# The stages behind attention, reordered by hand in a two-layer attention and expert kernel

## The chip, the cores and the metric

The kernel runs on one core of a Trainium2 chip. The metric is the device time of one execution in microseconds (us), as the median of several runs; lower is better. Engines are called TensorE (PE in the profile; PEld is its weight load), VectorE (DVE), ScalarE (ACT), GpSimd (POOL) and SyncE (SP, which issues most of the DMAs).

## The reference

Four sublayers on x of shape (4, 512, 128), each followed by a residual and a layer norm (cut to the core; biases are kept, small helpers are left out):

```python
# 1: attention with relative positions, 8 heads of 16
score = (einsum(q + u_bias, k) + rel_shift(einsum(q + v_bias, p))) / sqrt(128)
x = layernorm(x + softmax(score) @ v @ Wo + bo)
# 2: eight experts, top 1 (D=128, F=512)
xn = x * rsqrt(mean(x*x) + 1e-6) * rms_w
ye = silu(xn @ W1[e] + b1[e]) @ W2[e] + b2[e]      # e = argmax of xn @ gate_w
x = layernorm(x + ye * max(softmax(logits)))
# 3: gated convolution (3 taps) with a recurrence along the sequence, 256 wide
u = silu(conv(layernorm(x) @ W_in[:, :256])) * sigmoid(gate)
a, b, c = sigmoid(u @ Wa + ba), sigmoid(u @ Wb + bb), tanh(u @ Wc + bc)
state = a_t * state + b_t * u_t ;  y_t = c_t * state + u_t
x = layernorm(x + x + y @ Wo + bo)
# 4: fourteen experts, top 1 (D=128, F=256), gelu
x = layernorm(x + softmax(logits)[e] * (gelu(x @ w1[e] + b1[e]) @ w2[e] + b2[e]))
```

All data is float32.

## The kernel before

The four batches form two groups, (0, 1) and (2, 3). Tokens lie on the partitions in four tiles of 128 per batch, or, transposed, features on the partitions and 512 tokens along the free dimension. A float32 matmul takes two passes of TensorE, a transpose one.

**Attention** (function `attention`, L936) goes through 64 steps of two heads: scores (L643), softmax (L661 to L670), the flip of the probabilities one step or two later (L678, L680), and the product with V (L691). The engines' order in this part is the order of the program (`tc.manual_schedule`). Other work is cut into generators in the list `side`; each step calls each of them twice, and `room` says how many PSUM banks the step may lend them. `tiles_end` (L697) normalises and projects a pair of tiles, `attn_end` (L734) does the layer norm, the RMS norm, the routing and, for the last batch of a group, the dispatch. `experts(0, 0, ...)`, the layer-0 experts of the first group, is appended at step 49.

**Routing** (`route`, L277) takes the logits (L292), the largest, an Exp for the shares (L300) and the choice. **Dispatch** (L332) counts the tokens of each expert with matmuls (L354 to L356), gives each token a slot and writes the rows to their slots in DRAM (`sent`) with one indirect DMA of GpSimd per tile of 128 tokens (L386). A group of 1024 tokens has a block of 128 slots for each expert and 7 overflow blocks, whose expert is known only on the chip: 15 blocks in layer 0, 21 in layer 1.

**Experts** (L765) load blocks of rows in sets of four (L799), transpose them (L807), and for each block do an up projection (L822), bias (L829), the nonlinearity (layer 0: Tanh at L835 and a product at L842, layer 1: Gelu at L838), a down projection (L852) and a copy (L861); a set of four goes to DRAM (`made`, L864). Weights come through the tile `wd` (L787): 6 buffers with 4 loads ahead for the first group in layer 0, 3 and 3 for all others; 512 KB a block in layer 0. In layer 1 the weights of the fourteen experts are kept on the chip (`w1p`, `w2p`) and only overflow blocks load.

**Behind attention** no order is written out for the engines: the program calls one function after the other (L1133 to L1143), and the framework schedules its instructions. `layer0_end` (L1033) gathers the results with four indirect DMAs per batch (`collect`, L1023), takes two normalisations in a row, each with its own power on GpSimd (`rsqrt_of`, L229), and transposes. `recurrence` (L1060) does the convolution (L1071), its Sigmoid (L1073), the gate (L1076, L1078), the three gates of the recurrence (L1087, L1089), the scan (L1091), the output projection (L1098) and the routing of layer 1. `layer1_end` gathers and writes the output.

```python
    for b in GROUPS[0]:
        layer0_end(b)
    in_turns(recurrence(0), recurrence(1))
    drain(experts(1, 0, mid, None, None, W1_0, W2_0, E0, F0, "b1_0", col("rms_w")))
    drain(dispatch(0, x3, E1, F1, "b1_1", 1))
```

Batches 2 and 3 follow in the same way, then `second(0)`, a dispatch and `second(1)`, the layer-1 experts of each group with their ends.

Of the kernel before, what the change touches and what calls it, by code (L numbers as in the profile page):

```python
# [63 lines left out]
def tile_kernel(ctx: ExitStack, tc: tile.TileContext, x, wpack, cols, rows, tabs, b2bd0, b2bd1,  # L64
# [10 lines left out]
    small = pool(ctx, "small", 3)  # L75
# [7 lines left out]
    psum_a = pool(attn_psum, "psum_a", 1, **psum_of)  # L83
    prep_ctx = ExitStack()
    even = pool(prep_ctx, "even", 1)
# [50 lines left out]
    minus_half = const.tile([P, NT], F32, name="minus_half")  # L136
# [21 lines left out]
    def later_constants():  # L158
# [11 lines left out]
        def counting(name, pattern, base=0, channel_multiplier=0):  # L170
            shape = [P, *(n for _, n in pattern)]
            whole = const.tile(shape, I32, name=f"{name}i")
            nc.gpsimd.iota(whole, pattern=pattern, base=base, channel_multiplier=channel_multiplier)
            t = const.tile(shape, F32, name=name)
            nc.gpsimd.tensor_copy(t, whole)
            return t
# [13 lines left out]
    now, room = [None], [0]  # L190

# [31 lines left out]
    def rsqrt_of(src, n, eps, name, engine=None):  # L223

        engine = engine or nc.vector
        v = small.tile([P, n], F32, tag=f"var{n}", name=f"var_{name}")
        engine.tensor_scalar(v, src, eps, None, ALU.add)
        y = small.tile([P, n], F32, tag=f"rstd{n}", name=f"rstd_{name}")
        nc.gpsimd.tensor_tensor(y, v, minus_half, ALU.pow)  # L229
        t = small.tile([P, n], F32, tag=f"root{n}", name=f"root_{name}")  # L230
        engine.tensor_tensor(t, y, y, ALU.mult)
        engine.tensor_tensor(t, t, v, ALU.mult)
        engine.tensor_scalar(t, t, -0.5, 1.5, ALU.mult, ALU.add)
        engine.tensor_tensor(y, y, t, ALU.mult)
        return y

# [9 lines left out]

    def stats_of(src, name, engine=None):

        mean, var = moments(src, name)
        return mean, var, rsqrt_of(var, NT, 1e-5, name, engine)  # L250
# [14 lines left out]
    def transposed(src, name):  # L265

        pt = ps(name)
        for n in range(NT):
            nc.tensor.transpose(pt[:, n * P : (n + 1) * P], src[:, n, :], ident)  # L269
        return pt  # L270
# [4 lines left out]
    chosen, shares, slots, extra = {}, {}, {}, {}  # L275

    def route(xT, weights, n_e, b, layer, out):  # L277
# [4 lines left out]
        if at == 0:  # L282
            n_t = len(GROUPS[gr]) * NT
            chosen[layer, gr] = plan.tile([P, n_t, n_e], F32, tag=f"chosen{layer}_{gr}", name=f"chosen{nm}")
        mine = chosen[layer, gr][:, at : at + NT, :]
        w = small.tile([P, NT, 32], F32, tag="w", bufs=2, name=f"w{nm}")
# [4 lines left out]
        for n in range(NT):  # L291
            nc.tensor.matmul(lg[:, n, :], lhsT=xT[:, n * P : (n + 1) * P], rhs=weights, start=True, stop=True)  # L292
        yield
# [6 lines left out]
        nc.scalar.activation(ex, ex, AF.Exp)  # L300
# [3 lines left out]
        nc.vector.tensor_tensor(mine, eq, over(first, n_e), ALU.is_equal)  # L304
        yield
        yield
# [8 lines left out]
    def b2_of(w, b2t, b, layer, dst, base):  # L315
# [4 lines left out]
        nc.tensor.transpose(pw, w.rearrange("p n e -> p (n e)"), ident)  # L320
        yield
        wT = small.tile([P, P], F32, tag="wT", bufs=2, name=f"wT{nm}")
        nc.scalar.copy(wT, pw)
        yield
        yield from bank()
        pb = ps(f"pb{nm}")
        nc.tensor.matmul(pb, lhsT=wT, rhs=b2t, start=True, stop=True)
        yield
# [3 lines left out]
    def dispatch(gr, rows_of, n_e, n_f, b1, layer):  # L332
# [10 lines left out]
        eq = chosen[layer, gr]  # L343
        yield

        cum = brief("cum", [P, GT + 1, n_e], f"cum{nm}")
        nc.vector.memset(cum[:, 0, :], 0.0)
        for n in range(GT):
            nc.vector.tensor_tensor(cum[:, n + 1, :], cum[:, n, :], eq[:, n, :], ALU.add)
        yield  # L350
# [5 lines left out]
        nc.tensor.matmul(flat, lhsT=ones, rhs=cum[:, :GT, :].rearrange("p n e -> p (n e)"), start=False, stop=True)  # L356
        rank = flat.rearrange("p (n e) -> p n e", e=n_e)
# [16 lines left out]
        yield  # L374
        yield
# [7 lines left out]
        yield  # L383
# [10 lines left out]
        yield  # L394

# [7 lines left out]
        yield  # L403
        yield
# [12 lines left out]
        yield  # L417
# [59 lines left out]
    def attn_prep(b):  # L477
# [9 lines left out]
        apply_norm(xh, xs[b], mean, rsqrt_of(var, NT, 1e-5, f"a{b}", engine), engine)  # L487
# [106 lines left out]
        yield  # L594
# [5 lines left out]
    right_keys = [odd_even.tile([P, NG, S], F32, name=f"KR{i}") for i, odd_even in enumerate((even, odd))]  # L600
# [96 lines left out]
    def tiles_end(b, t2):  # L697
# [32 lines left out]
        if t2 == 1 and b < B - 1:  # L730
            side.insert(0, attn_end(b))
        yield

    def attn_end(b):  # L734

        engine = nc.vector if b == B - 1 else nc.gpsimd
        x1[b] = keep.tile([P, NT, D], F32, tag="x1", name=f"x1_{b}")
        yield
        mean, var, rstd = stats_of(xs[b], f"b{b}", engine)
        apply_norm(x1[b], xs[b], mean, rstd, engine)  # L740

        ms = small.tile([P, NT], F32, tag="ms", name=f"ms{b}")
        engine.tensor_tensor(ms, var, rstd, ALU.mult)
        engine.tensor_tensor(ms, ms, rstd, ALU.mult)
        rr = rsqrt_of(ms, NT, 1e-6, f"r{b}", engine)
        xf = keep2.tile([P, NT, D], F32, tag="xf", bufs=len(GROUPS[0]), name=f"xf{b}")
        xf_of[b] = xf
        for n in range(NT):
            engine.tensor_scalar(xf[:, n, :], x1[b][:, n, :], rr[:, n : n + 1], None, ALU.mult)
        for _ in range(4):  # L750
            yield
        yield
# [5 lines left out]
        yield  # L758
        w = []
        yield from route(xfT[b], colr("gate"), E0, b, 0, w)  # L760
        if b == GROUPS[GROUP[b]][-1]:
            yield from dispatch(GROUP[b], xf_of, E0, F0, "b1_0", 0)
        yield from b2_of(w[0], b2t0, b, 0, x1[b], x1[b])

    def experts(gr, layer, mid, w1t, w2t, W1, W2, n_e, n_f, b1, scale):  # L765
# [10 lines left out]
        def take(j):  # L776
# [10 lines left out]
            wd = mid.tile([P, 2 * n_f], F32, tag=f"wd{layer}", bufs=6 if within else 3, name=f"wd{nm}_{j}")  # L787
# [8 lines left out]
        def fetch(s):  # L796
            js = sets[s]
            rows_[s] = mid.tile([P, n_set, D], F32, tag="rows", name=f"rows{nm}_{s}")
# [3 lines left out]
        def turn(s):  # L802
# [3 lines left out]
            for k in range(len(js)):  # L806
                nc.tensor.transpose(pt[:, k * P : (k + 1) * P], rows_[s][:, k, :], ident)  # L807
            return pt

        def turned(s, pt):  # L810
            n = len(sets[s]) * P
            xts[s] = mid.tile([P, n_set * P], F32, tag="xt", name=f"xt{nm}_{s}")
# [5 lines left out]
        def up(j):  # L818
            xt = xts[j // n_set]
            ups[j] = ph = experts_psum("ph", f"ph{nm}_{j}")  # L820
# [4 lines left out]
        def bent(j):  # L825
            ph = ups.pop(j)
            hb = mid.tile([P, nf, P], F32, tag=f"hb{layer}", bufs=4 if within else 3, name=f"hb{nm}_{j}")
# [18 lines left out]
        def down(m):  # L846
            js = range(m * n_down, min((m + 1) * n_down, nblocks))
            py = experts_psum("py", f"py{nm}_{m}")
# [6 lines left out]
            def then():  # L855
                s = sets[js[0] // n_set]
                if js[0] == s[0]:
                    ys[js[0] // n_set] = mid.tile([P, n_set, D], F32, tag="ys", name=f"ys{nm}_{m}")
# [9 lines left out]
        ahead = 4 if within else 3  # L868
# [48 lines left out]
        yield  # L917
        yield
        yield from run(ops)

    def drain(gen):
        for _ in gen:
            pass
# [3 lines left out]
    side = []  # L927
# [8 lines left out]
    def attention(first, last):  # L936

        for k in range(first, last):
# [32 lines left out]
            if due is not None and due[2] == 1 and due[1] % 2 == 1:  # L971
                side.insert(0, tiles_end(due[0], due[1] // 2))

    def experts_psum(tag, name):
        return ps(name) if psum_e is None else psum_e.tile([P, 512], F32, tag=tag, name=name)

    psum_e = None
    begun = (B - 1) * NT * H // 2
    by_hand = {mybir.EngineType.PE, mybir.EngineType.DVE, mybir.EngineType.Activation, mybir.EngineType.Pool}
    with tc.manual_schedule(engines=by_hand):  # L980
# [4 lines left out]
        attention(0, begun + 1)  # L985
    prep_ctx.close()
    first_ctx = ExitStack()
    side.append(experts(0, 0, pool(first_ctx, "first", 2), None, None, W1_0, W2_0, E0, F0, "b1_0", col("rms_w")))
    with tc.manual_schedule(engines=by_hand):
        attention(begun + 1, len(steps) + 6)  # L990
    now[0] = None
    attn_psum.close()
    psum_e = pool(ctx, "psum_e", 3, **psum_of)
    for gen in side:
        drain(gen)
    first_ctx.close()
    mid = pool(ctx, "mid", 2)
    one = pool(ctx, "one", 1)
    drain(attn_end(B - 1))


# [249 lines left out]
```

## Time and profile before

| | us |
|---|---|
| median of 3 runs | 691.08 (687.99 to 693.28) |
| the profiled execution, device time | 696.16 |
| its span, first to last instruction | 694.5 |
| mean granted TensorE clock | 0.858 of full speed |

In the rows of the profile, a number behind x is a count, the first two numbers of a timeline row are start and length in us, and square brackets hold the idle time of the engine before the row and what ended it. In a table of stretches each engine has its busy time and, in brackets, the number of its instructions; then come the granted clock, the DMA engines' busy share and GB/s. Busy times overlap between engines.

### The profile page before, as it was taken

To read this page: it belongs to the slowest core of one execution; us is meant where nothing else is said; L and a number is where in the kernel's file an instruction comes from. 1 tells how busy PE (TensorE), PEld (TensorE's weight loads), DVE (VectorE), ACT (ScalarE), POOL (GpSimd) and SP (SyncE) were. 2 spreads that over 40 slices of the span, in tenths; PEclk is the share of its full clock that TensorE was granted. 3 is DMA by queue.
4 is the path that set the end of the run, shared out by engine and by line. 5 is a ranking of instruction groups with operands and counts; after the bars stand their busy time and mean duration, and the time that the engine had idled before them with its cause. 6 is when DMAs were issued, how large, how long until landed. Compare 5 with 4: busy or idle time off the path is not lost.

```text
span 694.5 us, 11212 instructions
## 1 busy us (share of the span) xinstructions
PE 505.2 (73%) x4060; PEld 352.9 (51%) x4060; DVE 366.3 (53%) x997; ACT 286.2 (41%) x573; POOL 177.9 (26%) x310
## 2 busy tenths in 40 slices
PE   5988979898989859988930797687605894873840
PEld 2455646575666537767920334486602343763830
DVE  2786747655675836573753356345334364342413
ACT  1256545655565635664301332332203333540621
POOL 1572411513141311500157100005053001027014
PEclk9989999989998988999965899578856996896895
DMA  9290131400040070209741000047610000255231
GB/s 321 75 279 16 32 76 16 92 2 1 14 96 1 21 216 24 73 2 246 239 133 60 1 0 0 1 117 219 207 42 0 0 1 0 64 156 150 68 117 53
DMA packets 71366, 56.16 MB, mean 81 GB/s; under 512 B 4624, under 2 KB 64400, under 8 KB 71056
## 3 DMA queue, kind: packets, MB, share of 16 engines
q1 hardware_dynamic: 69264, 51.25, 26.5%
q0 software_dynamic: 2048, 4.20, 1.9%
q8 instruction: 32, 0.52, 0.3%
q14 instruction: 22, 0.18, 0.1%
HBM read 36.30 MB, written 12.58 MB: 70 GB/s over the span
## 4 chain that ended last, share of the span: by engine, by line
PE 45%; DVE 17%; POOL 11%; DMA 8%; issue 8%; ACT 6%; SPq 2%; POOLq 0%; DVEq 0%; ACTq 0%
PE pa L1087 6%; PE py L852 5%; PE ptr L678 5%; PE ph L822 5%; PE ctx L691 4%; DVE nmax L666 4%; PE main L643 4%; PE pj L1071 3%; PE aux L643 3%; POOL back L1023 3%; DMA wd<-in_W_dram 2%; DMA back<-made,at 2%; DVE main L663 2%; DVE main L661 2%; PE pl L292 2%
## 5 line engine op out<-in xcount | busy, mean ns | idle before, releaser
L670 ACT ACTIVATE pr<-main,nmax 128x512 f32<-128x512 f32 x128 | 81.1, 686 | 52.2 <-DVE nmax L666 51.8
L678 PE MATMUL ptr<-ident,pr 128*128 128x128 f32 x512 | 86.5, 294 | 20.4 <-ACT prT L680 5.0
L680 ACT COPY prT<-ptr 128x512 f32<-128x512 f32 x128 | 74.2, 588 | 54.2 <-PE ptr L678 53.4
L678 PEld LDWEIGHTS ptr<-ident,pr 128*128 128x128 f32 x512 | 58.3, 147 | 62.0 <-issue 14.6
L666 DVE TENSOR_REDUCE nmax<-main 128x2 f32<-128x1024 f32 x64 | 78.3, 1224 | 2.2
L661 DVE COPY_PREDICATED main<-low,aux 128x256 f32<-128x256 uint32 x64 | 27.4, 428 | 76.8 <-PE aux L643 75.8
L822 PE MATMUL ph<-xt,wd 128*128 128x128 f32 x296 | 45.3, 299 | 13.3 <-DMA wd<-in_W_dram 12.0
L852 PE MATMUL py<-wd,hb 128*128 128x128 f32 x296 | 45.5, 301 | 5.5 <-ACT hb L838 3.0
L1023 POOL DMA_INDIRECT back<-made,at x32 | 32.7, 1021 | 65.4 <-DMA made<-ys 50.3
L822 PEld LDWEIGHTS ph<-xt,wd 128*128 128x128 f32 x296 | 39.8, 208 | 16.7 <-issue 8.7
L643 PE MATMUL aux<-Ko,QLo 32*128 32x128 f32 x480 | 44.9, 306 | 2.7 <-DMA Ko<-K 2.7
L852 PEld LDWEIGHTS py<-wd,hb 128*128 128x128 f32 x296 | 40.4, 211 | 8.6 <-ACT hb L838 4.5
L1087 PE MATMUL pa<-u,wabct 128*128 128x512 f32 x96 | 41.7, 594 | 1.7 <-ACT sg L1078 1.7
L691 PE MATMUL ctx<-prT,V 128*32 128x128 f32 x1024 | 39.5, 301 | 3.3 <-ACT prT L680 3.3
L269 PE MATMUL pgx<-ident,gxh 128*128 128x128 f32 x16 | 5.1, 451 | 50.1 <-DVE gxh L1045 50.1
L643 PE MATMUL main<-KR,QR 32*128 32x512 f32 (+3 forms) x192 | 40.6, 500 | 0.0
L829 DVE TENSOR_TENSOR hb<-ph,colt 128x256 f32<-128x256 f32 (+1 forms) x44 | 22.8, 519 | 32.5 <-PE ph L822 25.4
L643 PEld LDWEIGHTS aux<-Ko,QLo 32*128 32x128 f32 x480 | 33.1, 194 | 3.5 <-issue 3.5
L691 PEld LDWEIGHTS ctx<-prT,V 128*32 128x32 f32 x1024 | 29.3, 120 | 10.3 <-ACT prT L680 5.4
L386 POOL DMA_INDIRECT sent<-x,at x16 | 16.8, 1048 | 68.9 <-DVE pick L408 39.7
L835 ACT ACTIVATE th<-hb 128x512 f32<-128x512 f32 x30 | 18.9, 630 | 36.9 <-DVE hb L829 35.7
L269 PEld LDWEIGHTS pgx<-ident,gxh 128*128 128x128 f32 x16 | 3.2, 200 | 55.1 <-DVE gxh L1045 53.4
(293 smaller groups left out, 969.3 us busy)
## 6 DMA issues: line engine op xcount, KB each, us to landing
wd<-in_W_dram SPq DMA_DIRECT2D x60, 256.0 KB, 4.8
rows<-sent SPq DMA_DIRECT2D x16, 256.0 KB, 3.2
made<-ys SPq DMA_DIRECT2D x16, 256.0 KB, 2.6
wd<-in_W_dram SPq DMA_DIRECT2D x28, 128.0 KB, 2.3
sent<-zero SPq DMA_DIRECT2D x2, 1344.0 KB, 10.8
tab<-in_tabs_dram SPq DMA_DIRECT2D x2, 1280.0 KB, 9.1
Ko<-K SPq DMA_DIRECT2D x8, 256.0 KB, 4.3
QLo<-QL SPq DMA_DIRECT2D x8, 256.0 KB, 4.0
```

The lines of the kernel that those rows point to most:

```text
L643: nc.tensor.matmul(out, lhsT=Q[r, h // 4, q], rhs=K[r, h // 4, k0:k1], start=True, stop=True)
L661: nc.vector.copy_predicated(main[:, :, c0 : c0 + P], low.bitcast(U32).unsqueeze(1).to_broadcast([P, 2, P]), aux[:, :, 0, :])
L666: nc.vector.tensor_reduce(nmax, main, AX.X, ALU.max, negate=True)
L670: nc.scalar.activation(pr, main[:, i, :], AF.Exp, bias=nmax[:, i : i + 1])
L678: nc.tensor.transpose(ptr[:, c * P : (c + 1) * P], pr[:, c * P : (c + 1) * P], ident)
L680: nc.scalar.copy(prT.rearrange("p c q -> p (c q)"), ptr)
L691: nc.tensor.matmul(pc[32 * i : 32 * i + 32, :P], lhsT=V[:, c, 4 * g + i, :], rhs=prTs[i][:, c, :], start=(c == 0), stop=(c == NT - 1))
L822: nc.tensor.matmul(ph[:, fc * P : (fc + 1) * P], lhsT=weights[j][0][:, fc * P : (fc + 1) * P], rhs=xt[:, j % n_set * P : (j % n_set + 1) * ...
L829: nc.vector.tensor_tensor(hb, ph[:, : nf * P].rearrange("p (c t) -> p c t", t=P), bias.unsqueeze(2).to_broadcast([P, nf, P]), ALU.add)
L852: nc.tensor.matmul(py[:, k * D : (k + 1) * D], lhsT=hT[:, fc, :], rhs=weights[j][1][:, fc, :], start=(fc == 0), stop=(fc == nf - 1))
L1023: nc.gpsimd.indirect_dma_start(out=back[:, n, :], out_offset=None, in_=made[layer, gr][:, :], in_offset=bass.IndirectOffsetOnAxis(ap=slots ...
L1087: nc.tensor.matmul(pa, lhsT=wabct[:, k, kc, i * P : (i + 1) * P], rhs=u[kc], start=(kc == 0), stop=(kc == 1))
```

## The change

- The four compute engines get a written order behind attention too. Generators are given out by `play`: of those that are due, the first in a list always goes on. `spend` counts matmul work as it is given out, and a generator that yields a number rests until that many units were spent.
- Two main streams: `rest_of_last` (end of attention for batch 3, second group's layer-0 experts, its ends, its layer-1 experts), first in the list, and `rest_of_first`. Recurrences and the first group's layer-1 experts are appended behind them, the layer-1 ends are put in front.
- One expert pool `mid` from step 41 on. Weights of layer 0: 4 buffers, 3 ahead; layer 1: 3 buffers, 2 ahead; `rows` one buffer instead of two. The recurrence's tiles take the places of attention's.
- One power for two roots: of var + e and of var(1 + d) + de. The RMS-normed rows come straight from the attention output; they are made on VectorE, the layer-normed rows on GpSimd.
- Sigmoids are written with tanh. The convolution's sum first goes through an Identity on ScalarE; `ga` is halved and shifted on GpSimd. The factors 2 and 4 that this leaves in u go into scales. The Exp of the layer-1 routing becomes a Tanh with a quotient on VectorE.
- The sums over earlier tiles are taken with each batch's routing, the dispatch comes before the shares, and the dispatch of the first group begins the first expert stream itself instead of step 49. `attn_end(1)` stays ahead of `tiles_end` in the list.
- Attention stops 3 steps behind the last scores instead of 6.

```diff
+    def play():
+        while givers:
+            for giver in givers:
+                if giver[0] <= given[0]:
+                    wait = next(giver[1], "end")
+                    if wait == "end":
+                        givers.remove(giver)
+                    else:
+                        giver[0] = given[0] + (wait or 0)
+                    break
+            else:
+                given[0] = min(giver[0] for giver in givers)
...
+    def rstds_of(var, eps, name, engine):
+        v = small.tile([P, 2, NT], F32, tag="var", name=f"var_{name}")
+        engine.tensor_scalar(v[:, 0, :], var, 1e-5, None, ALU.add)
+        engine.tensor_scalar(v[:, 1, :], var, 1.0 + eps, 1e-5 * eps, ALU.mult, ALU.add)
+        y = newton(v, 2, name, engine)
+        return y[:, 0, :], y[:, 1, :]
...
-            wd = mid.tile([P, 2 * n_f], F32, tag=f"wd{layer}", bufs=6 if within else 3, name=f"wd{nm}_{j}")
+            wd = mid.tile([P, 2 * n_f], F32, tag=f"wd{layer}", bufs=(4, 3)[layer], name=f"wd{nm}_{j}")
...
-        ahead = 4 if within else 3
+        ahead = (3, 2)[layer]
...
+        yield from pause(3, sent_at[layer, gr] + 70 - given[0])
...
-            nc.scalar.activation(u[i], pc, AF.Sigmoid, bias=cbias[:, i : i + 1])
-            nc.vector.scalar_tensor_tensor(u[i], pc, cbias[:, i : i + 1], u[i], ALU.add, ALU.mult)
+            nc.scalar.activation(u[:, i, :], pc, AF.Identity, bias=cbias[:, i : i + 1])
+            nc.scalar.activation(sg[:, i, :], u[:, i, :], AF.Tanh, scale=0.5)
+            nc.vector.scalar_tensor_tensor(u[:, i, :], sg[:, i, :], 1.0, u[:, i, :], ALU.add, ALU.mult)
...
+                if k == 0:
+                    nc.gpsimd.tensor_scalar(ga[:, i, :], ga[:, i, :], 0.5, 0.5, ALU.mult, ALU.add)
...
+    def rest_of_last():
+        yield from tiles_end(B - 1, 1)
+        yield from attn_end(B - 1)
+        yield from experts(1, 0, W1_0, W2_0, E0, F0, "b1_0", col("rms_w"))
+        while 1 not in gxs:
+            yield 2
+        backs = [gather(b, 0) for b in GROUPS[1]]
+        yield 40
+        for b, back in zip(GROUPS[1], backs):
+            yield from layer0_end(b, back)
+            while b - 2 not in over_with:
+                yield 2
+            begin(recurrence(b), -1)
+        yield from layer1(1)
+
+    with tc.manual_schedule(engines=by_hand):
+        begin(rest_of_last())
+        begin(rest_of_first([gen for gen in side if gen.__name__ != "tiles_end"]))
+        play()
```

## The prediction

> **What bounds the kernel now.** I read the page first: span 694.5 us, device time of that execution 696.16 us; the three timed runs have the median 691.08 (687.99 to 693.28), 0.7% below it. The sum below is made against the span; 1.7 us lie around it, and at the end I scale by 691.08/696.16 = 0.993.
>
> ```profile
> PE 505.2 (73%) x4060; PEld 352.9 (51%) x4060; DVE 366.3 (53%) x997; ACT 286.2 (41%) x573; POOL 177.9 (26%) x310
> ...
> PE 45%; DVE 17%; POOL 11%; DMA 8%; issue 8%; ACT 6%; SPq 2%; POOLq 0%; DVEq 0%; ACTq 0%
> ```
>
> TensorE holds less than half of the chain that ended last, so the mean tells little. I then had the busy time cut at the borders of the stages (attention's last context matmul ends at 327).
>
> ```profile
> core 0: us, PE busy (x) PEld busy (x) DVE busy (x) ACT busy (x) POOL busy (x), PEclk, DMA share, GB/s
> 0.00:327.00 327.00, 277.88 (x2911) 189.38 (x2915) 202.50 (x430) 171.19 (x315) 93.57 (x212) 0.94 0.31 82
> 327.00:357.00 30.00, 25.09 (x212) 22.46 (x204) 19.43 (x67) 9.16 (x20) 6.65 (x7) 0.94 0.72 213
> 357.00:380.00 23.00, 0.38 (x1) 0.00 (x0) 10.32 (x64) 1.65 (x4) 17.73 (x24) 0.50 0.28 88
> 380.00:430.00 50.00, 42.52 (x120) 20.44 (x120) 25.46 (x54) 17.95 (x27) 2.85 (x6) 0.93 0.00 0
> 430.00:451.00 21.00, 11.15 (x31) 6.79 (x32) 7.40 (x48) 6.67 (x15) 2.44 (x4) 0.54 0.00 1
> 451.00:504.00 53.00, 40.95 (x262) 37.68 (x260) 24.63 (x53) 15.22 (x33) 8.82 (x8) 0.83 0.61 178
> 504.00:530.00 26.00, 1.95 (x7) 1.34 (x7) 12.48 (x62) 4.24 (x10) 15.50 (x20) 0.56 0.10 28
> 530.00:576.00 46.00, 41.60 (x115) 19.40 (x113) 21.90 (x39) 15.65 (x22) 0.00 (x0) 0.95 0.00 0
> 576.00:597.00 21.00, 11.47 (x35) 7.08 (x36) 7.72 (x49) 7.12 (x16) 2.02 (x2) 0.59 0.00 0
> 597.00:623.00 26.00, 22.97 (x191) 21.76 (x190) 12.72 (x42) 15.69 (x48) 2.67 (x3) 1.00 0.45 133
> 623.00:634.00 11.00, 0.08 (x1) 0.00 (x0) 0.64 (x2) 0.28 (x1) 8.34 (x9) 0.65 0.51 157
> 634.00:671.00 37.00, 29.13 (x189) 26.56 (x189) 14.33 (x55) 17.82 (x56) 7.03 (x7) 0.83 0.40 115
> 671.00:694.50 23.50, 0.00 (x0) 0.00 (x0) 6.75 (x36) 3.56 (x9) 10.32 (x10) 0.57 0.17 47
> ```
>
> The reader is to see that the 367 us behind attention go one stage after another. The two recurrences (380 and 530) are dense; between them TensorE is idle or sparse in 357 to 380 and 504 to 530 (rows come back, two normalisations), 430 to 451 and 576 to 597 (x3 and routing), 623 to 634 (scatter, rows). Yet the group of batches 0 and 1 doesn't depend on the other: this idle time is order, not need. Two more views show what sits inside.
>
> ```profile
> 482.84 1.06 PE L852 MATMUL py<-wd,hb 128*128 128x128 f32 x8
> 484.80 1.13 PE L822 MATMUL ph<-xt,wd 128*128 128x128 f32 x8 [0.91 <-DMA wd<-in_W_dram]
> 485.76 1.06 PE L852 MATMUL py<-wd,hb 128*128 128x128 f32 x8
> ```
> ```profile
> 363.34 1.03 POOL L386 DMA_INDIRECT sent<-xf,at  x1 [0.17 <-DVE oneb L414]
> ...
> 372.44 0.98 POOL L386 DMA_INDIRECT sent<-xf,at  x1 [0.30 <-issue]
> 373.42 1.08 POOL L229 TENSOR_TENSOR rstd_c<-var_c,minus_half 128x4 f32<-128x4 f32 x1
> ```
>
> An up and a down projection of a layer-0 block start 0.96 us apart, 1.9 us for both, but a block comes only every 3 us or so (484.80 to the next at 487.87), because it waits for its weights. And POOL issues a burst of eight row DMAs in 10.4 us (1.3 each); the power for a root stood behind such a burst.
>
> **The change, part by part.** *Unit.* The new order counts matmul work. A unit is 0.22 us: a 512-wide fp32 matmul is 4 units and takes two passes of 0.435 (48 passes of the gates in 20.87 us). So its pauses of 35, 40 and 70 units are 7.7, 8.8 and 15.4 us.
>
> *Up to attention's end.* Scatter and expert pool of the first group come some 2 to 4 attention steps earlier (4.6 us each), which takes the wait of 7.2 us for its first rows (at 251.7) out of TensorE's queue; the first normalised rows move from POOL to DVE, 4 x 0.34 us in three batches, +4. The weight ring falls from 6 buffers to 4 while downs come in pairs: up(2m+4) must wait for a load that starts when down(m) ends. The load takes 4.8 us (median of the 256 KB weight loads) plus 0.75 of issue = 5.5. Six pairs, 33 us, if nothing stands between; in attention only about one expert operation goes into a step, so 0 to 2 us remain in each of three pairs, and all of it in the three pairs behind attention. I take +3 in attention, and attention's end unchanged at 327.
>
> *327 to the experts of the second group.* TensorE holds the rest of the first pool, about 7 ups and 13 downs x 0.9 = 18 us, plus up to 15 of ring waits; the second group's normalisation, routing and ranks go between them. The shared root removes one power (1.0 us), its hand-overs and some nine DVE instructions of 0.16 us: about 3 us from this chain, and 2.7 from each normalisation behind layer 0. Pauses of 35, 6 and 10 units lie ahead of the scatter, some 76 units of the rest ahead of the first gather, so by my count the eight scatters now go ahead of the eight gathers: 360 to 370 instead of 363.3 to 373.4. Landing 2.2 and rows 3.2 follow, so this pool begins at 377 (369 to 385). It has strict precedence: the first recurrence, ready at about 380, stands behind it.
>
> *Second pool of layer 0.* Before: 53 us. Now 4 buffers, but down(j-2) follows up(j). A buffer is held for issue and landing (0.7 + 4.0 in this stage), two block periods and 1.9 us of matmuls, and this is four periods: T = 6.6/2 = 3.3 us. 3 x 1.9 + 12 x 3.3 + 2 = 47, to 424. The cover is gone here: what TensorE waits, nobody else uses.
>
> *Recurrences.* 48 + 16 + 96 wide passes stay. Per half, ACT gains one Identity, 0.69 us; DVE has three fused operations of 0.75 where it had 0.75, 0.69 and 0.69; POOL gains one conversion of 128x512. No row shows that one; the copy of this size took 0.61, the two-operand form 1.27, and I take 1.27. All lies beside 45 us of matmuls for two batches (ACT 17, DVE 21, POOL 5). The two-by-two order drops five waits of 0.8 for a sigmoid, so 45 instead of 50 and 42 instead of 46; 4 us of transposes and routing matmuls lie between. Four loads of 1.28 us (sigmoid, exp) go. The gathers and normalisations of batches 2 and 3, 26 us before, now lie beside the first recurrences, and x3 and routing of batches 0 and 1 (21) beside the others. What is late next: a conversion on POOL behind a burst, its scan on DVE, and what is queued behind that scan. Two bursts, each 10.4 us, against slack of two or three steps: I take 3 each, 0 to 10 as bounds. 424 + 45 + 42 + 4 + 6 = 521.
>
> ```profile
> L838 ACT ACT_TABLE_LOAD x1 | 1.3, 1283 | 0.0
> ```
>
> *A rule that speaks against this.* The row shows one load of 1.283 us when Gelu begins; exp loads at 441, and the tanh of the pool behind it (454) needs none, so these two share. Whether tanh after Gelu loads again no row shows; the bounds are 0 and two loads at each alternation, some six alternations, 15 us on ACT. I take 0 on the path, because ACT has 60% idle there.
> The Trainium skill, page "ScalarE: Activation LUTs", section "Table sets: the hidden batching unit", says to do all of one set before the next, and lists tanh with exp and with sigmoid but not with gelu. By that page the sum would have those 15 us more on ACT, and perhaps half of it on the path.
>
> *Last stages.* From the last recurrence to the rows of the second group in layer 1: x3 and routing 21, ranks and DVE 5, scatter 10.4, landing and rows 6, less the overlap with b2, 37. In it the first group's layer-1 pool must fit: 26 before, plus its ring. Three buffers with lag two: from the fourth overflow block on, each takes load 2.3 + issue 0.7 + two projections 0.9 = 3.9 us instead of 2.3, four blocks, +6. So 38, to 559. Then the last pool, 37 before, 4 less for a DVE wait at 641, +5 for the ring: 38, to 597. The end, gathers and norm, stays at 23.5: span 620.5. Plus 1.7, times 0.993: 618 us.
>
> **The rivals.** (a) POOL becomes the bound. 64 row DMAs are 83 us, and three bursts fall into recurrences whose scans now need POOL. Against it: 26% busy. If three bursts come through at 10 us each, +24 beyond my 6: 642, and 655 with a fourth and its gathers.
> (b) The pauses don't fit, and the gaps only move: the order is fixed, so a short pause leaves DVE in front of a gather. Then 26 (504 to 530), 21 (430 to 451) and 23 (574 to 634 is 60, taken as 37) return: 690.5, about 687, no change. For it: gather to rows takes 10.4 + 2.6, more than 8.8. Against it: the next pause follows, and POOL alone is late.
> (c) Slower: the weight ring. Its place is all four pools, 31 refilled blocks, where strict precedence lets nobody fill in, and in the first pool attention's own transposes stand behind the wait. My gain is 74 us, so it decides from 2.4 us a block beyond those I took. At 6.7, the longest landing of the second pool, with six pairs exposed and TensorE at the half clock that it shows from 357 to 380 (0.50), I get 3.5 a block, +108: about 725. Against it: DMA shares of 0.4 to 0.7 leave room, and attention spaces the first pairs.
>
> **How the numbers follow.** Forecast 0.62 (590 to 640); better than 590 by dense matmuls at full clock 0.04; (a) 0.20; (b) 0.05; (c) 0.09. 1% is about what this measurement tells from no change (the runs spread by 0.8%). Faster 0.86, same 0.05, slower 0.09. The range leaves out (b), (c) and the best tail: 590, where ring (3 + 6 + 5), POOL (6) and the late start (8) cost nothing, to 664, (a) with its upper bounds and the half of the first pool's exposed loads.
>
> **What would show it.** Right: second-pool blocks 3.3 us apart with waits for weights; one dense stretch of TensorE of 130 us or more behind it; sparse TensorE only around 355 and in the last 24 us; one power per normalisation; no sigmoid loads. Wrong: gate scans waiting for POOL, gathers seen as DVE's longest wait, weight waits above 5 us inside attention, an activation load at each turn between tanh and Gelu, attention ending past 335.

## The result, and the profile after

The changed kernel takes 721.0 us (median of 4 runs, 719.36 to 723.35) beside 692.18 of the kernel before on the same chip: ratio 1.044, 95% interval 1.038 to 1.050. One of the four runs of the kernel before, 704.0 us, fell in a slow state of the chip and is not in the ratio. The changed kernel is slower by 4.4%, where 618 us was forecast. The profiled execution has a span of 721.4 us and a granted clock of 0.842.

The busy times and the chain that ended last, from the page of the changed kernel:

```profile
PE 506.4 (70%) x4060; PEld 359.4 (50%) x4060; DVE 371.2 (51%) x979; ACT 282.3 (39%) x577; POOL 173.4 (24%) x287
...
PE 41%; DVE 22%; issue 11%; ACT 9%; DMA 8%; POOL 7%; SPq 1%; POOLq 0%; ACTq 0%; DVEq 0%
```

TensorE has as many matmuls as before and nearly the same busy time (506.4 against 505.2). No engine got more work that matters, and in the chain TensorE has a smaller share (41 instead of 45%) and VectorE a larger one (22 instead of 17%). What grew is the time in which TensorE has none: 215 us of the span instead of 189. Cut at the borders of the stages (end of attention, gap, second pool of layer 0, recurrences, layer-1 pool of the first group, gap, last pool, end):

```profile
core 0: us, PE busy (x) PEld busy (x) DVE busy (x) ACT busy (x) POOL busy (x), PEclk, DMA share, GB/s
0.00:320.00 320.00, 275.35 (x2976) 190.67 (x2977) 208.63 (x442) 173.21 (x321) 82.44 (x182) 0.96 0.32 89
320.00:378.00 58.00, 24.05 (x144) 20.73 (x142) 23.77 (x92) 5.69 (x13) 24.45 (x24) 0.68 0.43 120
378.00:425.00 47.00, 37.09 (x263) 33.93 (x263) 23.27 (x48) 16.77 (x39) 1.69 (x5) 0.89 0.53 156
425.00:573.00 148.00, 102.24 (x273) 50.56 (x271) 71.67 (x229) 45.98 (x84) 35.47 (x47) 0.82 0.05 16
573.00:635.00 62.00, 37.25 (x226) 34.45 (x226) 21.98 (x77) 19.10 (x57) 9.04 (x10) 0.72 0.23 69
635.00:653.00 18.00, 0.00 (x0) 0.00 (x0) 3.53 (x18) 2.08 (x5) 9.22 (x9) 0.57 0.31 91
653.00:697.00 44.00, 30.45 (x185) 29.06 (x185) 11.74 (x39) 16.17 (x52) 1.00 (x1) 0.69 0.27 80
697.00:721.40 24.40, 0.00 (x0) 0.00 (x0) 6.61 (x36) 3.29 (x8) 10.10 (x10) 0.50 0.18 55
```

Up to 425 all is as forecast (424). The 101 us by which the span is above the forecast's 620.5 all come behind it: recurrences 148 instead of 97 (+51), first layer-1 pool 62 instead of 38 (+24), a gap of 18 that the forecast didn't have, last pool 44 instead of 38 (+6), the rest +2. In the 148 us no engine is busy for more than 102: the engines wait for each other. The timeline of all engines (start, length, engine, line, operation) shows how:

```profile
463.22 0.65 PE L308 MATMUL pgx<-ident,back 128*128 128x128 f32 x4
...
468.03 1.02 POOL L258 TENSOR_TENSOR rstd_h<-var_h,minus_half 128x4 f32<-128x4 f32 x1 [9.28 <-DVE var_h L269]
...
470.13 1.65 ACT L301 ACTIVATE x<-gxb,shift_h,rstd_h 128x128 f32<-128x128 f32 x4 [4.96 <-DVE shift_h L299]
471.69 0.76 ACT L1107 ACTIVATE gxnT<-pgx,colt 128x512 f32<-128x512 f32 x1
...
472.50 5.04 PE L1127 MATMUL pj<-gxnT,wconv 128*128 128x512 f32 x6 [7.78 <-ACT gxnT L1107]
```

One recurrence begins: its transposes `pgx` are done at 463.9, and it needs one copy on ScalarE, `gxnT`. But `gxnT` was given out behind `x`, the output norm of the recurrence before it. That norm goes by VectorE, one power on GpSimd, five small VectorE operations and then ScalarE. ScalarE has nothing to do for 4.96 us, with a ready instruction second in its queue; TensorE, which has matmuls for the recurrence that follows, waits 7.78. The Trainium skill, page "PSUM — Partial Sum Buffer", section "Engine vs sequencer instructions", says that the queues of ScalarE, VectorE and GpSimd are strictly first in, first out; these rows agree. The gap before the last pool is the same thing, from the timeline of TensorE and of ScalarE:

```profile
634.11 0.60 PE L859 MATMUL pxs<-ident,rows 128*128 128x128 f32 x4
653.09 2.08 PE L876 MATMUL ph<-xt,w1p 128*128 128x128 f32 x8 [18.39 <-ACT xt L867]
```
```profile
650.92 1.65 ACT L301 ACTIVATE res<-res,shift_d,rstd_d 128x128 f32<-128x128 f32 x4 [16.29 <-DVE shift_d L299]
652.47 0.56 ACT L867 COPY xt<-pxs 128x512 f32<-128x512 f32 x1
```

The rows that the last pool begins with are transposed at 634.7. Their copy `xt` takes 0.56 us, and it stands behind the end of batch 0 in layer 1, which was given out first and waits for its gathers and a power. TensorE's largest waits behind attention, from the view of waits from 320 on (total us, times, longest):

```profile
PE pw L379 <- DVE w L371: 33.3, 5, 8.1
PE ph L876 <- DMA wd<-in_W_dram: 29.7, 18, 3.3
PE ph L876 <- ACT xt L867: 23.9, 3, 18.4
PE pgx L308 <- DVE back L293: 16.0, 1, 16.0
```

`pw` transposes the routing's shares, which come out of a row of small VectorE operations. Its waits are the largest here (33.3 us; the same wait took 4.3 us in the kernel before), and they show VectorE's queue. One case, from the timeline of all engines:

```profile
612.08 0.26 DVE L418 TENSOR_TENSOR more<-rank,over 128x98 f32<-128x98 f32 x1 [4.97 <-PE rank L412]
...
617.76 0.18 DVE L363 TENSOR_SCALAR den<-ex 128x56 f32<-128x56 f32 x1
...
619.66 0.45 PE L379 MATMUL pw<-ident,w 128*128 128x128 f32 x1 [7.61 <-DVE w L371]
```

The first step of the shares is `den`. Its input `ex` left ScalarE at 603.6 (L348). But the change puts the dispatch ahead of the shares, so `den` stands behind 21 VectorE operations of the dispatch, and the first of them waits 4.97 us for TensorE's ranks while VectorE does nothing. `den` comes 14 us after it was ready; with the shares, VectorE goes through 27 operations in a row from 612.1 to 619.5, and TensorE's next matmuls stand behind the transpose `pw`.

### The profile page after: what moved, and what is told of

It reads as the page before. It is cut to its first block, busy times and chain, and to the rows that moved or that the text cites. A ratio compares the mean times of both kernels' runs of the same rounds, so it can differ in the third digit from the quotient of the medians.

```text
span 721.4 us, 11161 instructions
## 1 busy us (share of the span) xinstructions
PE 506.4 (70%) x4060; PEld 359.4 (50%) x4060; DVE 371.2 (51%) x979; ACT 282.3 (39%) x577; POOL 173.4 (24%) x287
## 4 chain that ended last, share of the span: by engine, by line
PE 41%; DVE 22%; issue 11%; ACT 9%; DMA 8%; POOL 7%; SPq 1%; POOLq 0%; ACTq 0%; DVEq 0%
DMA wd<-in_W_dram 6%; PE ptr L730 6%; PE ph L876 6%; PE py L907 5%; PE ctx L743 4%; PE main L695 4%; PE pa L1146 4%; DVE nmax L718 4%; PE aux L695 3%; POOL back L1075 2%; DVE main L715 2%; DVE main L713 2%; ACT pr L722 1%; DMA made<-ys 1%; POOL sent L441 1%
## 5 line engine op out<-in xcount | busy, mean ns | idle before, releaser
L730 PE MATMUL ptr<-ident,pr 128*128 128x128 f32 x512 | 84.6, 291 | 18.8 <-ACT prT L732 3.6
L732 ACT COPY prT<-ptr 128x512 f32<-128x512 f32 x128 | 74.1, 587 | 47.1 <-PE ptr L730 46.2
L876 PE MATMUL ph<-xt,wd 128*128 128x128 f32 x296 | 49.5, 316 | 35.0 <-DMA wd<-in_W_dram 32.1
L876 PEld LDWEIGHTS ph<-xt,wd 128*128 128x128 f32 x296 | 42.7, 220 | 40.1 <-issue 19.0
L907 PEld LDWEIGHTS py<-wd,hb 128*128 128x128 f32 x296 | 42.1, 220 | 6.5 <-DVE hb L896 4.3
L743 PE MATMUL ctx<-prT,V 128*32 128x128 f32 x1024 | 37.9, 293 | 8.0 <-ACT prT L732 7.4
L876 PE MATMUL ph<-xt,w1p 128*128 128x128 f32 x112 | 21.8, 333 | 23.9 <-ACT xt L867 23.9
L743 PEld LDWEIGHTS ctx<-prT,V 128*32 128x32 f32 x1024 | 28.2, 116 | 15.0 <-ACT prT L732 11.2
L883 DVE TENSOR_TENSOR hb<-ph,b1x 128x512 f32<-128x512 f32 (+1 forms) x28 | 15.5, 555 | 36.6 <-PE ph L876 31.2
L892 ACT ACTIVATE hb<-hb 128x256 f32<-128x256 f32 x42 | 17.4, 415 | 42.6 <-DVE hb L883 42.6
L1146 PE MATMUL pa<-gKo,wabct 128*128 128x512 f32 x48 | 28.8, 744 | 5.2 <-DVE gKo L1139 5.2
```

What stands on the lines that cost most here:

```text
L730: nc.tensor.transpose(ptr[:, c * P : (c + 1) * P], pr[:, c * P : (c + 1) * P], ident)
L732: nc.scalar.copy(prT.rearrange("p c q -> p (c q)"), ptr)
L743: nc.tensor.matmul(pc[32 * i : 32 * i + 32, :P], lhsT=V[:, c, 4 * g + i, :], rhs=prTs[i][:, c, :], start=(c == 0), stop=(c == NT - 1))
L876: nc.tensor.matmul(ph[:, fc * P : (fc + 1) * P], lhsT=weights[j][0][:, fc * P : (fc + 1) * P], rhs=xt[:, j % n_set * P : (j % n_set + 1) * ...
L883: nc.vector.tensor_tensor(hb, ph[:, : nf * P].rearrange("p (c t) -> p c t", t=P), bias.unsqueeze(2).to_broadcast([P, nf, P]), ALU.add)
L907: nc.tensor.matmul(py[:, k * D : (k + 1) * D], lhsT=hT[:, fc, :], rhs=weights[j][1][:, fc, :], start=(fc == 0), stop=(fc == nf - 1))
```

## The experiments

The theory (A): the written order behind attention is the loss. Four engines with a fixed order, in which one stream's chain stands in front of another's ready work, lose more than the overlap gains. The main rival (B) is the weight ring of the prediction's case (c); a second is the tanh form. Each chip timed the kernel before beside the runs (698.6 for e1 to e4, 693.4 for e5 to e8 and 699.0 us for e9 to e12), so ratios are compared; 0.01 is 7 us. The expectations are in us; where a chip was faster or slower, the text says what the ratio makes of it.

**The framework orders the tail (e1), and a batch's ends are given out later (e2), and the two recurrences of a group are given out in turns (e3).**

```diff
-    with tc.manual_schedule(engines=by_hand):       # e1
+    with ExitStack():
...
-        yield 40                                    # e2: layer1_ends
+        yield 40 if gr else 130
...
-            begin(recurrence(b))                    # e3: rest_of_first, likewise (2, 3) in rest_of_last
+        begin(in_turns(recurrence(0), recurrence(1)))
```

> The changed kernel, with one thing undone: behind attention the four engines' order is again made by the framework from the same program (the generators still give the work out in the same sequence). Theory A, the written order itself is the loss, because a chain of one stream stands in the queues of VectorE and ScalarE ahead of another stream's work: the stretch between the second pool and the first layer-1 pool (148 us, 425 to 573) falls to 100 to 120, and the time to 650 to 685. Rival B, the weight ring: the waits for wd (32 us) stay, the time stays at 705 to 721. Rival C, the added work (Identity, conversions on GpSimd, tanh): 715 to 721.

> The changed kernel, with the first group's two layer-1 ends given out 130 units of matmul work after their gathers instead of 40, so behind most of the last pool's blocks. Theory A: the wait of 18.4 us of TensorE for xt at 653, behind the end of batch 0 on ScalarE, goes, and a few us come back inside the pool: 703 to 709. Rivals B and C: no part of this is touched, and the 18 us come back as a wait for rows or weights: 718 to 722.

> The changed kernel, with the two recurrences of a group given out piece by piece in turns, as before the change, instead of the first one ahead of the second. If strict precedence between them is a main cause (each gate waits for its own u, 3 to 5 us at a time, and for the clock that falls with it), the stretch of 148 us falls by 15 to 30 and the time to 690 to 706. If the normalisation chains in the queues are the cause and not the sequence of the two, 712 to 724.

Measured: e1 653.61 us, ratio 0.938 (0.932 to 0.944). With the same instructions and buffers and only their order left to the framework, the kernel is 6% faster than before instead of 4% slower: 0.106 of ratio, 74 us, is the written order. Theory A expected this (650 to 685); both rivals expected 705 us or more. Its stretches from the second pool on:

```profile
core 0: us, PE busy (x) PEld busy (x) DVE busy (x) ACT busy (x) POOL busy (x), PEclk, DMA share, GB/s
...
376.00:420.00 44.00, 33.19 (x247) 31.29 (x247) 22.36 (x40) 17.93 (x41) 3.72 (x9) 0.88 0.59 167
420.00:534.00 114.00, 93.76 (x287) 46.78 (x285) 68.37 (x222) 44.98 (x84) 32.82 (x38) 0.93 0.07 21
534.00:577.00 43.00, 29.35 (x222) 26.88 (x222) 17.27 (x74) 18.46 (x56) 8.88 (x9) 0.92 0.31 95
577.00:627.00 50.00, 32.49 (x189) 30.06 (x189) 14.70 (x57) 18.25 (x55) 10.08 (x10) 0.72 0.37 107
627.00:650.90 23.90, 0.23 (x2) 0.00 (x0) 6.77 (x36) 3.57 (x9) 10.35 (x10) 0.50 0.20 58
```

The recurrences fall from 148 to 114 us and the first layer-1 pool from 62 to 43; the gap of 18 is gone, but the last pool (50) is longer than the 44 before it. The waits for `pw` go from 33.3 to 4.8, the 18.4 for `xt` is gone; the weights keep about their size, and the wait for the first normalised rows in the gap before the second pool (`pgx`) is longer, 25.4 instead of 16.0 (view from 315 on):

```profile
PE ph L876 <- DMA wd<-in_W_dram: 28.2, 21, 3.6
PE pgx L308 <- DVE back L293: 25.4, 1, 25.4
...
PE pw L379 <- DVE w L371: 4.8, 1, 4.8
```

e2: 713.57 us, ratio 1.024 (1.006 to 1.042), 14 us below the changed kernel; the 18.4 us wait is no longer there (all waits of that kind together 6.2). Its interval is wide (two runs, 708.5 and 718.7) and overlaps that of the changed kernel, so the size is rough; by the ratio it is 707 us beside the first chip's 691, inside the 703 to 709 of theory A, and as it stands 713.6 lies between the two expectations. e3: 702.2, ratio 1.009 (1.004 to 1.013), 25 us below the changed kernel, as expected for strict precedence as a main cause (690 to 706). So a third of the loss goes when neither recurrence of a group stands ahead of the other. The edit does one thing more: a pair begins only when both of its batches are normalised, and the second pair only when both of the first are through. What that alone does was not run.

**The kernel before, with its tail in its own written order (e4).** Its calls of the ends, recurrences, experts and dispatches are put under the same manual schedule, their order as written.

```diff
+    with tc.manual_schedule(engines=by_hand):
+        for b in GROUPS[0]:
+            layer0_end(b)
+        in_turns(recurrence(0), recurrence(1))
...
```

> The kernel before, with one thing added: the part behind the last layer-0 normalisation of attention keeps the order of its own program on the four engines instead of the framework's. Theory A: the framework's reordering is worth a lot here, so 720 to 770. If a written order costs nothing by itself: 688 to 698.

811.42 us, ratio 1.164 (1.158 to 1.171). So what looked like stages one after another in the profile of before had already been moved about by the framework, and this was worth 113 us, more than theory A expected (720 to 770 us). Its two largest waits on TensorE are those for the normalisations (50.1 us in the kernel before) and for weights (12.0 before):

```profile
PE pgx L269 <- DVE gxh L1045: 77.0, 4, 27.3
PE ph L822 <- DMA wd<-in_W_dram: 52.9, 20, 3.0
```

The changed kernel, with its generators and its other parts, is 0.120 of ratio better than this (1.164 to 1.044, 84 us of 699), and loses to the framework all the same.

**Whose queue (e9 to e12).** One engine alone in the written order, the three others free.

```diff
-    with tc.manual_schedule(engines=by_hand):
+    with tc.manual_schedule(engines={mybir.EngineType.PE}):      # e9; DVE e10, Activation e11, Pool e12
```

> The changed kernel with TensorE's order alone as the generators give it; VectorE, ScalarE and GpSimd are ordered by the framework behind attention. The whole written order costs about 67 us (721 against 654). Theory A (the loss is made in the queues of the engines that serve TensorE: one batch's steps stand in them ahead of another batch's that are ready): most of the 67 us is gone, 655 to 680. Rival (it is TensorE's own order that is bad, matmuls of a later stream stand behind one that waits): 695 to 720, and the order on the other engines hardly matters.

> The changed kernel with VectorE's order alone as written. Theory A: VectorE has the most instructions of the recurrences and routings, and where its order is fixed, a waiting step of one batch holds all others: 675 to 710. Rival (TensorE's own order): 650 to 665.

> The changed kernel with ScalarE's order alone as written. Theory A: ScalarE's queue is the second place of the loss (the copy of gathered rows stood 16 us behind the end of batch 0): 665 to 695. Rival (TensorE's own order): 650 to 665.

> The changed kernel with GpSimd's order alone as written. Theory A: GpSimd is busy for a quarter of the time, its order gives little of the loss: 650 to 665. Rival (GpSimd's powers, gathers and scatters in a fixed order hold the others, the forecast's case of GpSimd as the bound): 670 to 700.

| written order on | us | ratio (95%) | above e1's ratio, x 699 us |
|---|---|---|---|
| none (e1) | 653.61 | 0.938 (0.932 to 0.944) | 0 |
| GpSimd (e12) | 654.16 | 0.934 (0.930 to 0.939) | -2 |
| ScalarE (e11) | 667.83 | 0.957 (0.951 to 0.962) | 13 |
| TensorE (e9) | 669.17 | 0.959 (0.953 to 0.965) | 15 |
| VectorE (e10) | 687.00 | 0.986 (0.980 to 0.992) | 33 |
| all four (the change) | 721.0 | 1.044 (1.038 to 1.050) | 74 |

VectorE's queue alone makes nearly half of the loss; ScalarE's and TensorE's make 13 to 15 each. All four lie where theory A expected them, and each is outside its rival's range, though ScalarE's only by 3 us. The four sum to 59; the other 15 would come only when all are fixed together, but each ratio is known to about 0.006 (4 us) and e1's enters this difference three times, so 15 is no more than its noise. GpSimd's order costs nothing, so the case of GpSimd as the bound (a) falls in this form. With VectorE alone fixed, the waits on routing's shares come back on TensorE:

```profile
PE pw L379 <- DVE w L371: 14.3, 3, 6.6
```

**What remains in the free order (e5 to e8).** e5 lets the first group's gathers wait until the second group's routing has its slots. e6 gives the ring of layer 0 five buffers. e7 computes the recurrence's sigmoids by Sigmoid, without the conversions and factors of the tanh form (the routing keeps its tanh). e8 is e1, e2, e5 and e6 together.

```diff
+        while (0, 1) not in slots:                  # e5: rest_of_first, ahead of the gathers
+            yield 2
...
-            wd = mid.tile([P, 2 * n_f], F32, tag=f"wd{layer}", bufs=(4, 3)[layer], name=f"wd{nm}_{j}")   # e6
+            wd = mid.tile([P, 2 * n_f], F32, tag=f"wd{layer}", bufs=(5, 3)[layer], name=f"wd{nm}_{j}")
...
-        ahead = (3, 2)[layer]
+        ahead = (4, 2)[layer]
...
-                nc.scalar.activation(gates[k][:, i, :], pa, AF.Tanh, scale=scale,      # e7, one of its lines
-                                     bias=col("bc", i) if k == 2 else half_bias[:, k + 1, i : i + 1])
-                if k == 0:
-                    nc.gpsimd.tensor_scalar(ga[:, i, :], ga[:, i, :], 0.5, 0.5, ALU.mult, ALU.add)
+                nc.scalar.activation(gates[k][:, i, :], pa, AF.Tanh if k == 2 else AF.Sigmoid,
+                                     bias=col(("ba", "bb", "bc")[k], i))
```

> The changed kernel with the framework's order behind attention (653.6 us) and one thing more: the gathers of group 0's recurrence are begun only when the second group's routing has its slots, so that its eight scatters stand ahead of those gathers in POOL's queue. Theory A (the stretch between the pools is held by the order on POOL, eight indirect DMAs of about 1.0 us each): the second pool begins about 8 us earlier (368 instead of 376), and the end comes 5 to 8 us earlier, 645 to 649. Rival (the scatters wait for routing's own arithmetic and not for the gathers, so that the change only delays the recurrences): 653 to 662, with the gap on TensorE unchanged at about 25 us.

> The changed kernel with the framework's order behind attention (653.6 us) and five instead of four buffers for the expert weights of layer 0, loads one further ahead. TensorE waits 28.2 us for weights there, in both pools of layer 0 and in layer 1. Rival B (the one shared ring for the experts is a large part of what was lost): a buffer more takes 10 to 18 us of these waits, 636 to 644, and the weight waits fall to 10 to 18. Theory A (the weights' waits are small steps beside the order): the waits fall by less than half, 645 to 653.

> The changed kernel with the framework's order behind attention (653.6 us), and the recurrence's sigmoids computed by the Sigmoid function instead of tanh, with the arithmetic that came with the tanh form (the conversion on POOL, the factors of two) left out. Theory A (tanh in place of sigmoid saves loads of 1.28 us each and costs 16 POOL conversions of 0.62 us that lie beside other work): 4 to 10 more loads in ScalarE's rows, 655 to 670. Rival (the tanh form's extra arithmetic costs what it saves): 645 to 655, whatever the number of loads.

> The changed kernel with four edits together: the framework's order behind attention, the scatters of the second group ahead of group 0's gathers, five weight buffers for layer 0, and group 0's layer-1 ends given out later. Theory A: the written order is the loss and the other parts of the change are gains; what remains of waits is divided among them, 630 to 645, below both kernels. If the wider ring and the scatters each only move the waits elsewhere: 648 to 655, the same as with the framework's order alone.

e5: 643.57 us, ratio 0.931 (0.922 to 0.940), 4.5 us below e1 with overlapping intervals. The second pool's rows do come earlier, by 13 us, but part of it is given back at once. In TensorE's timeline of e5:

```profile
363.10 1.09 PE L859 MATMUL pxs<-ident,rows 128*128 128x128 f32 x4 [16.28 <-DMA rows<-sent]
...
375.93 2.07 PE L907 MATMUL py<-wd,hb 128*128 128x128 f32 x8 [5.90 <-DVE hb L896]
```

The rows are transposed at 363 instead of 376, and then the pool waits 5.9 us for VectorE. A gain for the end of 5 us is likely, not shown: on e1's chip the ratio is 650.5 us, between what the theory (645 to 649) and the rival (653 to 662) expected.

e6: 640.12, ratio 0.927 (0.919 to 0.936), some 7 us below e1, with intervals that still overlap. TensorE's waits for weights from 315 on fall from 28.2 to 16.9 us, by 40%:

```profile
PE ph L876 <- DMA wd<-in_W_dram: 16.9, 12, 2.7
```

That fits both expectations (10 to 18 us left, and a fall by less than half), and the time does not choose either: 640 is in the rival's range, but on e1's chip the ratio is 648, in the theory's. In the profiled execution the first recurrence begins 15.7 us earlier than in e1 (406.6 against 422.3). The second pool takes 37.9 us of it instead of 46.2, which gives 8.3; the other 7.4 were there before, as the pool's rows come at 368.7 instead of 376.1. In e6 attention ends 5.7 us earlier than in e1, but as early (318) as in the changed kernel with four buffers, so the earlier start need not be the ring.

e7: 647.23, ratio 0.933 (0.925 to 0.941), the same as e1. In its rows of ScalarE there is one table load more than in e1, which has those at L487 and L892 alone; 4 to 10 more were expected. That expectation was wrong, the rival's held:

```profile
L487 ACT ACT_TABLE_LOAD x1 | 1.3, 1283 | 0.8 <-PEq L1328 0.8
L1131 ACT ACT_TABLE_LOAD x1 | 1.3, 1283 | 0.0
L892 ACT ACT_TABLE_LOAD x1 | 1.3, 1283 | 0.0
```

L1131 loads when the sigmoids begin (425.5), and the tanh of the gates behind it (442.6 to 523.0) needs no other load. The tanh form of the recurrence gains and costs nothing that can be measured here.

e8: 631.63 us (628.52 to 632.45), ratio 0.911 (0.903 to 0.918). This version beats both kernels, by 9% the one before, and is 0.027 of ratio (19 us) below e1, with intervals apart.

## Why the prediction was wrong

- **Up to attention's end, 327 to the second pool, second pool of layer 0**: right in the sum, in part by luck. Attention's last context matmul starts at 318.0 instead of 327.3, which the forecast didn't expect; the gap behind it is longer by as much, and the second pool begins at 378 (forecast 377). It takes 47 us (47), but its blocks come 2.8 us apart (385.5 to 419.2 for twelve), not 3.3; a slower start and end make up for it. Two details more were wrong. The eight gathers went ahead of the eight scatters (354 to 364, then 365 to 375), against my count. The ring's share inside attention was 2.4 us of weight waits on TensorE (32.1 in all, 29.7 of it behind 320), against +3.
- **Recurrences** is the step that failed: 97 us forecast, 148 measured. The 97 were 91 us of matmuls and 6 for late conversions. Of the 148, TensorE is busy for 102 and idle for 46, so the term of 6 is what failed. The matmuls were sized nearly right: in the free order TensorE is busy for 94 of the 114 us, and for 82 of the 95 us from 420 to 515, though that dense stretch is 95 us long and not the 130 that I named. That the gathers and normalisations of batches 2 and 3 "now lie beside the first recurrences, and x3 and routing of batches 0 and 1 (21) beside the others" took it for granted that two streams on TensorE also overlap on VectorE and ScalarE. In a written order they do so only where the order interleaves them, and strict precedence puts each chain of short dependent steps as one piece in front of the next stream (27 on VectorE where the dispatch stands ahead of the shares). That the dispatch before the shares could cost anything was not in the forecast. e1 gives 34 of the 51 us back. The other 17 lie in the last recurrence and a routing, which have little left to lie beside (in e1, 19 us from 515 to 534 with waits of 6.5 and 4.8); I had hidden them too. The matmul sum itself was tight by some 2 us: it drops five waits of 0.8 us for a sigmoid per pair, where the timeline of before has four of 0.8 to 0.9.
- **What is late next** was sought on the wrong engine: I priced a conversion on GpSimd behind a burst of row DMAs (6 us). The conversions took 0.62 us each, not the 1.27 taken, and GpSimd's order costs nothing (e12). VectorE (33) and ScalarE (13) were the queues to walk through. On VectorE I named only a scan behind such a conversion and, in rival (b), a step in front of a gather; on ScalarE no instruction that would stand behind a waiting one, as `gxnT` and `xt` did.
- **Last stages**: 62 instead of 38 for the first layer-1 pool, and 18 for a gap. Of these 42 us e1 shows 37 gone, and gives 6 back in the last pool (50 instead of 44). The forecast's pauses were read as times at which work is ready; the end of batch 0 was given out 40 units after its gathers, and ScalarE waited 16 us for it in front of `xt`.
- **Weight ring**: in the second pool right in the sum (47 us with refill waits). In all pools, 29.7 us of waits behind attention; in the free order (28.2) a fifth buffer takes back 11 of them and about 7 us of time. As a rival for a slower kernel (c) it was the wrong mechanism: 725 us came out near the measured 721 by luck, from another cause, for e1 with the same ring is faster than before.
- **Rival (b), the gaps only move**, was nearest to what happened, with 0.05. It was priced as the old gaps coming back and no more (687); the written order also opened new ones, and the reason against it, "POOL alone is late", was never tested on VectorE and ScalarE. The deeper fault is that I read the stages of before as the order its program gives, and so the idle time between them as free to take. e4 shows the framework had already earned 113 us there; an order written by hand starts from that debt.
- **The rule on table sets** (the Trainium skill, "ScalarE: Activation LUTs", "Table sets: the hidden batching unit"): it lists tanh with exp and with sigmoid but not with gelu, so by it tanh behind Gelu would load again. In the trace of the changed kernel there are two loads in all, one at the beginning and one at Gelu's beginning (573.7); the routing's tanh at 603.4, between Gelus, needed none. Taking 0 was right. The six alternations that I counted were in fact one, because the gates were done when Gelu began.
- **Shared root**: one power per normalisation came as said, but with eight columns it takes 1.64 to 1.70 us, where four columns took 1.03; so it saves 0.4 us of GpSimd's time and not 1.0. The rows of the two-root power and of the conversions in the changed kernel (least, median, longest ns):

```profile
L258 POOL TENSOR_TENSOR rstd_c<-var_c,minus_half x4: 1636/1658/1696, 374.7 to 476.2; 128x8 f32<-128x8 f32 x4
```
```profile
L1152 POOL TENSOR_SCALAR gV<-gV x4: 614/617/618, 483.7 to 568.0; 128x512 f32<-128x512 f32 x4
```

Of the 30 us that e1 is still above the forecast's span (650.9 to 620.5), 17 are the last recurrence and routing, 17 the two layer-1 pools (43 and 50 instead of 38 each), less 4 by which the recurrences begin earlier. What is open: whether the four orders cost more together than one by one (the 15 us that noise can make), and why the second pool of e6 starts earlier.

## What to carry to other kernels

Before an order is written by hand, run the same program with that order taken away, and the old one with its own order fixed: the difference is what the framework already gives, and it has to be beaten first. A count of matmul work says when TensorE is free, not when a chain over VectorE, GpSimd and ScalarE is done; walk through each of these queues at every hand-over and ask which ready instruction stands behind one that waits. By the table, VectorE's order is the dearest of the four when it alone is fixed; that freeing VectorE alone would gain most was not run.

## What the runs showed of the hardware

- Idle time on TensorE costs a second time. Four layer-1 matmuls take 0.61 us in a dense stretch and 1.06 just behind a pause of 4.7 us; in the changed kernel's timeline of TensorE it takes 6 us to come back:

```profile
590.29 1.22 PE L876 MATMUL ph<-xt,w1p 128*128 128x128 f32 x4 [4.68 <-ACT xt L867]
591.30 1.06 PE L907 MATMUL py<-w2p,hb 128*128 128x128 f32 x4
...
596.87 0.61 PE L907 MATMUL py<-w2p,hb 128*128 128x128 f32 x4
```

  In the recurrences the granted clock is 0.82 in the written order and 0.93 in the free one. Over the whole kernel the same 4060 matmuls are busy for 506.4 us in the written order and 484.9 in e1: 21 of the 70 us between the two spans (721.4 and 650.9) are not waits, but matmuls that run slower.
- A power on GpSimd grows with its columns (1.03 us for 128x4, 1.66 for 128x8), while a conversion of 128x512 takes only 0.62.
- Tanh runs behind Gelu (603.4, the load for Gelu at 573.7) and, in e7, behind Sigmoid (442.6, the load for Sigmoid at 425.5) without a table load of its own.
